# A pointwise convolution computed from seven quarter products, its weights loaded through a shared ring, and position terms of attention keys made once

## The chip, the core and the metric

The kernel runs on one core of a Trainium2 chip. The core has TensorE (PE: matrix products; its weight loads appear as PEld), VectorE (DVE), ScalarE (ACT), GpSimd (POOL) and SyncE (SP, which here issues nearly all DMAs). The time is that of one execution on the device in microseconds; the median of some runs is compared. Everything is float32.

## The reference

Two layers work on x, an array of 8 images with 512 channels of 32 x 32 pixels. Layer 0 is a bottleneck block with attention, layer 1 a depthwise and a pointwise convolution. Each adds its result to its input, which is group-normalised (32 groups) on the way in. Cut to what matters:

```python
def layer0(x):                       # C = 256, 4 heads of 64, N = 2
    t = silu(bn(conv1x1(x, cv1_w)))  # 512 channels
    ys = [t[:, :C], t[:, C:]]
    for i in range(N):
        yi = ys[-1]
        z = silu(bn(conv3x3(yi, m_cv1_w[i])))
        q, k, v = conv1x1(z, m_qkv_w[i])
        r = m_rw[i] + m_rh[i]        # one term per column, one per row
        a = softmax(q @ (k + r) * HD ** -0.5)
        z = silu(bn(conv1x1(a @ v, m_cv2_w[i])))
        ys.append(yi + z)
    return silu(bn(conv1x1(concat(ys), cv2_w)))

def layer1(x):
    h = relu(bn(depthwise3x3(x) + dw_b))
    h = where(max(abs(h)) over the image < 4, 0, h)         # per channel
    h = relu(bn(conv1x1(h, pw_w) + pw_b))                   # 512 -> 512
    return where(max(abs(h)) over the image < 1e-3, 0, h)

x = x + layer0(group_norm(x));  x = x + layer1(group_norm(x))
```

## The kernel before

One image of 512 channels and 1024 pixels is held as four chunks of 128 partitions x 1024. All eight images run through one long instruction stream; the work of layer 1 for an image lies among that of layer 0 for the next image.

The order is written out by hand as strings. Each stage function puts its pieces into lists under short names (`add`, line 298), and `go` (301) takes pieces from the lists as the words of a plan say. `FIRST` (45) is image 0, `HEAD` (64) the first part of every later image (with layer 1 of the image before), `TAIL` (80) and `LAST` (87) the end of a middle image and of the last. `InOrder` (95) keeps every engine but POOL in exactly this order. So where a word stands decides what stands behind it on its engine's queue; because nearly all calls pass through the helper in line 105, the profile shows that line for most instructions and they are told apart by tiles.

Words that matter here:
- `c`, `y` with `ca`, `ya`: the first 1x1 convolution (`cv1`, 590) and its ends on ScalarE; `g gm gd gv gp gb ga` is the group norm ahead of it (429), with two tiny products on TensorE and a power on POOL.
- `d`, `P`, `Rc`, `R`, `B`, `E`, `Ez`: the 3x3 convolution in transformed form (`conv3`, 631). VectorE makes three components (`d`, twelve pieces, into `kr`, `vt` and `qy`), TensorE multiplies them with transformed weights (six `P`, one ring tile each), VectorE transforms back (`R`, `B`, `E`) and ScalarE ends it (`Ez`, into `z`). In image 0 the weights are transformed first (`ta`, `ti`, `to`, 313) and stored in DRAM.
- `k`, `ka`, `kp`, `v`, `va`, `q`, `qa`: keys, values and queries (787). A key chunk is ended in two steps, below.
- `s`, `e`, `p`, `w`: scores, exponentials, their sums over keys on VectorE, and products with values (857); `h`, `z`, `n`, `nr`, `ns`, `sc`, `nc`: joining halves, denominators, reciprocals, spreading them by DMA, scaling, and a range check on ScalarE.
- `m`, `ma`, `mr`: the 1x1 convolution after attention (963).
- `Q`, `K`, `r0` to `r3`, `u0`, `a0`, `x0` and so on: the last 1x1 convolution; in images 1 to 6 it is done with seven quarter products in place of eight (`quartered`, 1090), whose weight sums image 0 makes once (`cw`, `combine_weights`, 1059).
- `i`, `im`, `id`, `iv`, `ip`, `ib`, `b`, `bm`, `t`, `l`, `lr`, `lp`: layer 1 to the depthwise convolution and its pruning (486); its taps `t` are VectorE's.
- `o`, `oa`, `fr`, `f`: the pointwise convolution (531): products, ScalarE's normalisation, the largest value per channel, residual and store.

The pointwise convolution multiplies all four input chunks of `ht` by `wpw_sb`, a tile of 1 MB that stays in SBUF. Per image these are eight output banks (chunk m, half n) of four products each:

```python
nc.tensor.matmul(bank(m, n), wpw_sb[:, k, m * P : (m + 1) * P],
                 ht[k][:, n * 512 : (n + 1) * 512], start=(k == 0), stop=(k == KC - 1))
```

In the last image the pruning factor is multiplied into `wpw_sb` in place of `ht`, and the products are ordered by input chunk.

The keys get their position terms in two steps: VectorE adds the column term as it empties the bank (`columns`, 812), POOL then adds the row term in place (`lines`, 821).

Other weights pass through a ring of `NRING` = 4 tiles of 1 MB (`ring_sources`, 377, `ring_load`, 399): each product that empties a tile issues the next load on SP's queue. In image 0 the ring is held before the second layer's weights, which are not ready (`held`, word `rh`).

PSUM has two double banks (`ps_big`: scores, `P`, keys), three single banks (`ps_acc`: values, `m`, `o`, `y` and the quarter products) and one more (`ps_mm`). Work tiles of 128 x 1024 come from a pool of 11.

Of the kernel before, what the change touches and what calls it, by code (L numbers as in the profile page):

```python
# [10 lines left out]
F32 = mybir.dt.float32  # L11
# [18 lines left out]
NRING = 4  # L30
# [15 lines left out]
    g*4 gm g gd g gv g gp g gb ga gm gd gv ga c gp fo gb c ga ta0 ga ta0*2 ti0 fo ta2 ti0 ta2  # L46
    ti0 to0*2 c ca ta2 c rl ca ta1*3 ti1 to1*2 ti1*2 y ya y ti2 d*2 ya d ti2 to2 y ti2 to2 rl ya
    y d*3 ya P d Rc d R d*2 P Rc R d*2 P Rc R B*2 P Rc R P Rc R E P Ez B*2 Rc R E Ez X dw*2
    ta0*2 k*3 ka k kp ka ta0 v kp ti0 v va ti0 v ti0 v va ta1 q*2 qa ta1 q ta1 q qa s e s e p
    to0 s e p w to0 s e w*2 ti1*2 s e p ti1 p s e p w s*2 e p w to1 e w to1 p s e w ta2 s e w h  # L50
    z ta2 s e p*2 w ta2 s ti2 e p w s e w p ti2 s e w p ti2 to2 s e p w to2 s e p w s e w s e rh
    p w h z s e s w e p w s n e p w nr s e p w nr s nr e nc p s nr e ns w s e p w*2 nc s e p w h
    z s p e p s w s e s e w p sc e p*2 w sc s e p w*2 s e p w*3 h z n nr*4 ns Q nc*2 K sc dp sc
    m ma mr m ma mr m*2 ma mr ma mr Q d*3 K d*2 P d*4 P Rc R d Rc R d*2 P Rc R B*2 P Rc R B P B
    Rc R E Ez P Rc R E Ez k X dx k*3 ka*2 kp*2 v*2 q v*2 va*2 q qa q*2 qa s*2 e*2 p s e p w s
    cw*2 e w s p e s e w s e p cw*2 p w s e p*2 s e w s e w*2 p w h z s e w cw s e p cw s e w p
    w p g*2 s e p w s e w p s e g w s p g s w g*2 e*2 p w h z s e p s w e g p w s e p n w nr g
    nr s e s p w nr e s e p w nr s p e ns w nc w s e p w h s nc s e p w e p w s e p w z s e p w
    s sc e p w sc s e p w*3 h z n nr*2 Q nr*2 ns Q sc*2 nc m nc m ma mr ma mr m ma m ma mr gm mr
    gd Q gv u A Q x u i A x i gp i*2 Q gb ga*4 Q im id Q iv A Q x ip i*2 ib b bm t*3 Q A t*2 x  # L60
    i*2 t
# [3 lines left out]
    c*2 b im id bm c ca iv t ip t l t*2 lr ib b c bm ca b t y t*2 d y bm d ya d ya d*5 y P Rc ya  # L65
    R d*2 P Rc R d P d Rc R B P Rc R B P B Rc R E P Rc B Ez R E Ez y k*3 ya X k ka dp kp t lp ka
    t*2 kp t*2 v*2 va t l t v*2 va t*2 lr lp q*4 qa s qa s e*2 t p s t e w t p s e w p l s*2 w
    e*2 p w p s t e s w s e*2 w t s p e p w*2 h lr z s e p t w s e w s p s p e w*2 p s e*2 p w s
    t e s p*2 w s e w e t p w h z lp t s*2 e p e w s*2 n e w s p w nr s p e w p w nr e p nr e
    s*2 nr t p ns w*2 e*2 nc l lr p lp w nc h sc s*2 e z w*2 s e*2 p*2 s e p w*2 s e w s e p*2  # L70
    w*3 p h n o nr sc z nr*3 ns o oa o oa sc m sc oa m nc ma nc ma m ma mr m mr ma mr*2 d o d*3
    o d oa d o P d*2 Rc d*3 oa R P Rc d R oa fr P Rc P R B Rc B R f P Rc P B*2 Rc R*2 E o E Ez
    fr oa Ez o X f k oa fr f fr f dx k*2 ka k kp ka kp v*2 q va v*2 q*3 va qa*2 s e s*2 w e p e
    w p s e p w s*2 e*2 p*2 w s*2 e*2 w s g p e w*2 s e w p s*2 h g e g p z w s p w e*2 s w e
    g*2 s*2 w e w p e g p g p*2 s w*2 e p s e w h s*2 e*2 p z p w*2 s e p*2 n s w nr*2 g w nr e
    s e p w p s w e p s nc e nr w s ns e nc w s h s p w z e p w e p s e w s e p sc s w p e p w s
    sc e p w*3 h n nr*4 ns z
# [3 lines left out]
    nc r2 Q*2 K r0 Q sc Q m r0 r2 r0 sc nc K m*2 ma mr ma m r0 ma mr r1 Q r1 Q*2 ma mr r2 mr  # L81
    r1*2 u0 r2 a0 u1 gm a1 x0 gd Q x1 u0*2 r3 gv r3 gp r3 Q gb u0 r3 u0 Q u0 a0 ga a0 ga Q i*2
    x0*2 ga Q i u0 a0 i im id Q iv ip u1 x0 Q u1*2 ib u1 b a1 x1 bm Q ga u1 a1 t i t Q x1 u1 i
    a1 i t i t x1 t*2
# [3 lines left out]
    Q sc*2 nc*2 m ma m*2 ma m rg ma mr*2 ma mr*2 Q*2 A rg x i*2 Q im id iv ip ib b bm Q t Q A x  # L88
    i*2 Q im id t*3 iv ip t ib Q t b Q bm t*4 l lr t A Q x i*2 Q im lp id t iv ip t A ib t b bm
    Q t*2 A x t l lr x i*2 o lp o*4 im id t*2 o*2 iv ip t ib b bm o*2 t o*4 t o*3 t*2 l t lr t*2  # L90
    lp t*2 o t*2 o*5 t l o*2 lr lp o*3 oa*2 fr o f oa*2 fr f o*2 oa*2 o*2 fr f oa*2 fr f
# [34 lines left out]
def fast_kernel(  # L126
# [42 lines left out]
    pt = [const_tile([P, HW], f"pt{c}") for c in range(KC)]  # L169
# [22 lines left out]
    wpw_sb = const_tile([P, KC, C], "wpw_sb")  # L192
# [26 lines left out]

    raw = [[t.rearrange("p a b -> p (a b)")[:, : 6 * C2] for t in (qy, kr, vt)]]  # L220
# [7 lines left out]
    for l in range(2):  # L228
        for dy in range(3):
            load_raw(l, dy)  # L230

# [144 lines left out]

    def ring_sources():
        for b in range(B):
            for l in range(2):
                for i in range(6):  # L380
                    yield u_dram[l][i].rearrange("p a b c d -> p (a b c d)"), 2048
                yield wqkv[:, l].rearrange("p k o -> p (k o)"), 1536
                if b == l == 0:
                    for m in range(2):
                        yield w2[:, :, m * P : (m + 1) * P], 1024
            if 0 < b < B - 1:
                for i in range(2):
                    for p in range(2):
                        yield s_dram[p][i].rearrange("p q k o -> p (q k o)"), 512 * (3 + i)
                continue  # L390
            for m in range(KC):
                yield w2[:, :, m * P : (m + 1) * P], 1024

    sources = list(ring_sources())
    ring = []

    held = [len(sources) - 9, 0]

    def ring_load(n=1):
        for _ in range(n):  # L400
            if len(sources) <= held[0]:
                held[1] += bool(held[0])
                continue
            src = sources.pop(0)
            t = ringp.tile([P, 2048], F32, tag="ring", name="wring")
            o = t[:, : src[1]]
            if src[1] == 1024:
                o = o.rearrange("p (k o) -> p k o", o=P)
            nc.sync.dma_start(o, src[0])
            ring.append(t)  # L410
# [74 lines left out]

    def layer1_front(groups, last=False):
# [28 lines left out]
        def prune(c):  # L515
            positive(keep[c])
            if last:

                w = wpw_sb[:, c, :]
                nc.vector.tensor_scalar(w, w, keep[c], None, ALU.mult)  # L520
            else:
                nc.gpsimd.tensor_scalar(ht[c], ht[c], keep[c], 1.0, ALU.mult, ALU.mult)
# [8 lines left out]
    def layer1_back(b):  # L531
# [4 lines left out]
        def bank(m, n):  # L536
            if (m, n) not in banks:
                if b < B - 1:
                    banks[m, n] = bank_tile("ps_pw")
                elif m in (0, 3):  # L540
                    t = big_tile("ps_pw")
                    banks[m, 0], banks[m, 1] = t[:, 0, :], t[:, 1, :]
                elif (m, n) == (2, 1):
                    banks[m, n] = ps_mm.tile([P, 512], F32, tag="mm", name="ps_pw")
                else:
                    banks[m, n] = bank_tile("ps_pw")
            return banks[m, n]

        def part(m, n, ks):
            for k in ks:  # L550
                nc.tensor.matmul(
                    bank(m, n),
                    wpw_sb[:, k, m * P : (m + 1) * P],
# [5 lines left out]
        def close(m, n):  # L559
            if n == 0:  # L560
                box[m] = work_tile("pw")
            act(box[m][:, n * 512 : (n + 1) * 512], bank(m, n), AF.Relu, BN5 + m)
# [15 lines left out]
        if b < B - 1:  # L578
            add("o", *[lambda m=m, n=n: part(m, n, range(KC)) for m, n in every])
# [6 lines left out]
        add("oa", *[lambda m=m, n=n: close(m, n) for m, n in every])  # L586
# [199 lines left out]

    def qkv(l, by_input):
# [22 lines left out]
        full = [P, 4, F, F // 4]  # L810

        def columns(m):
            col = rw[:, l, m, :].rearrange("p (t r) -> p r t", r=4)
            nc.vector.tensor_tensor(
                phases(kr[:, m, :]),
                phases(flat(tiles.pop(m + 2))),
                col.unsqueeze(2).to_broadcast(full),
                ALU.add,
            )

        def lines(m):
            row = rh[:, l, m, :].unsqueeze(1).unsqueeze(3)
            kk = phases(kr[:, m, :])
            nc.gpsimd.tensor_tensor(kk, kk, row.to_broadcast(full), ALU.add)  # L824
# [24 lines left out]
        add("ka", *[lambda m=m: columns(m) for m in range(2)])  # L849
        add("kp", *[lambda m=m: lines(m) for m in range(2)])  # L850
# [238 lines left out]

    def quartered():  # L1090
# [128 lines left out]
    for b in range(B):  # L1219
        first, last = b == 0, b == B - 1  # L1220
        if first:
# [8 lines left out]
            add("rl", *[lambda: ring_load(2)] * 2)  # L1230
            add("dw", lambda: nc.sync.dma_start(wm2_sb, wm2), lambda: nc.sync.dma_start(wpw_sb, wpw))

            def released():
                held[0] = 0
                ring_load(held[1])

            add("rh", released)
# [481 lines left out]
```

## Time and profile before

| | |
|---|---|
| median of 3 runs | 2625.31 us (2624.21 to 2625.61) |
| profiled execution, its time | 2622.91 us |
| profiled execution, its span | 2621.1 us |
| TensorE busy | 2578.2 us, 98% |
| VectorE busy | 2020.8 us, 77% |
| ScalarE busy | 1179.0 us, 45% |
| POOL busy | 169.9 us, 6% |
| mean DMA rate | 90 GB/s |
| granted TensorE clock | 0.998 |
| one middle image (910.89 to 1230.35) | 319.46 us, TensorE busy 319.17, VectorE 250.16 |

The page gives, for each engine, the busy time and the number of instructions; then groups of instructions by what they write and read, with busy time, mean length of one and the idle time ahead of them. A float32 product is two records, each with its weight load. Records of one engine can overlap a little, so the spacing of their starts is shorter than their length. The view by stage gives busy times in a stretch; the timeline lists merged instructions by their start; a wait is given with the instruction that ended it. The profiled execution ran 2.4 us below the median of the runs.

### The profile page before, as it was taken

What the parts mean: (1) busy time and instruction counts of PE and PEld (TensorE: products, weight loads), DVE (VectorE), ACT (ScalarE), POOL (GpSimd) and SP (SyncE); (2) the same over time, 40 slices, a digit from 0 to 9 for tenths busy, and PEclk for the clock granted to TensorE, in tenths of its full rate; (3) what the DMA queues carried; (4) which work ended last, traced back from release to release, by engine and by line L of the source; (5) the groups of instructions that cost most, each with busy time, mean ns of one, the idle gap of its engine ahead of it and who ended that gap; (6) DMA issues with size and microseconds to landing.
All of it is one profiled execution on the core that took longest, in us unless ns stands there. A gap on an engine that the chain in (4) does not pass through costs nothing.

```text
span 2621.1 us, 36162 instructions
## 1 busy us (share of the span) xinstructions
PE 2578.2 (98%) x14862; PEld 1328.7 (51%) x14862; DVE 2020.8 (77%) x2844; ACT 1179.0 (45%) x1509; POOL 169.9 (6%) x99
## 2 busy tenths in 40 slices
PE   8999999999999999999999999999999999999997
PEld 5454464634646346463464635645355544646443
DVE  8876588766887778778787778876788767887557
ACT  3634446253453544525445354444445444363534
POOL 1000011000100001000010000100001000010000
PEclk9999999999999999999999999999999999999999
DMA  9443130402304113040130402304122131302200
GB/s 340 157 154 124 65 141 25 151 31 73 138 20 149 31 67 141 17 165 17 64 141 17 165 17 80 125 27 155 33 95 95 61 121 33 132 27 85 73 17 34
DMA packets 74238, 236.00 MB, mean 90 GB/s; under 512 B 6096, under 2 KB 34000, under 8 KB 59984
## 3 DMA queue, kind: packets, MB, share of 16 engines
q1 hardware_dynamic: 70512, 230.19, 25.2%
q10 hardware_dynamic: 3552, 3.41, 0.4%
q8 instruction: 119, 1.95, 0.3%
q14 instruction: 55, 0.45, 0.1%
HBM read 183.77 MB, written 33.03 MB: 83 GB/s over the span
## 4 chain that ended last, share of the span: by engine, by line
PE 90%; DVE 4%; ACT 3%; issue 1%; DMA 0%; POOL 0%; SPq 0%; POOLq 0%; DVEq 0%; ACTq 0%
PE ps_av L105 16%; PE ps_s L105 15%; PE ps_c L105 12%; PE ps_cv L105 10%; PE ps_qk L105 8%; PE ps_cv2q L105 8%; PE ps_pw L105 8%; PE ps_v L105 4%; PE ps_m L105 4%; PE ps_y L105 4%; PE ps_dn L105 1%; DVE ht L105 1%; ACT qy L105 1%; ACT e L105 0%; ACT over L105 0%
## 5 line engine op out<-in xcount | busy, mean ns | idle before, releaser
L105 ACT ACTIVATE e<-ps_s 128x1024 f32<-128x1024 f32 x512 | 510.6, 1023 | 272.7 <-PE ps_s L105 262.2
L105 PE MATMUL ps_s<-qy,kr 64*64 64x512 f32 x4096 | 537.9, 592 | 4.4 <-ACT e L105 3.1
L105 PE MATMUL ps_av<-e,vt 64*64 64x512 f32 x4096 | 536.3, 590 | 1.4 <-ACT part L105 0.7
L105 DVE TENSOR_TENSOR sum<-sum,e 128x1024 f32<-128x1024 f32 x384 | 472.8, 1231 | 61.4 <-ACT e L105 42.0
L105 DVE SCALAR_TENSOR_TENSOR ht<-xn,v_sb,ht 128x961 f32<-128x961 f32 (+1 forms) x256 | 326.7, 1283 | 8.5 <-ACT ht L105 5.0
L105 PEld LDWEIGHTS ps_av<-e,vt 64*64 64x64 f32 x4096 | 183.9, 133 | 271.2 <-issue 237.5
L105 PEld LDWEIGHTS ps_s<-qy,kr 64*64 64x64 f32 x4096 | 173.6, 132 | 281.5 <-issue 169.8
L105 PE MATMUL ps_pw<-ht,wpw_sb 128*128 128x512 f32 x512 | 226.7, 598 | 5.4 <-DVE wpw_sb L105 5.4
L105 PE MATMUL ps_qk<-z,wring 128*128 128x512 f32 x512 | 227.2, 593 | 2.7 <-ACT z L105 1.9
L105 DVE TENSOR_TENSOR sum<-e 128x1024 f32<-128x1024 f32 x64 | 78.2, 1223 | 162.7 <-ACT e L105 162.7
L105 PEld LDWEIGHTS ps_pw<-ht,wpw_sb 128*128 128x128 f32 x512 | 96.5, 191 | 127.8 <-issue 126.0
L105 ACT COPY c<-ps_c 128x256 f32<-128x256 f32 x96 | 35.7, 372 | 272.6 <-PE ps_c L105 239.2
L105 PEld LDWEIGHTS ps_qk<-z,wring 128*128 128x128 f32 x512 | 96.8, 190 | 115.3 <-issue 106.6
L824 POOL TENSOR_TENSOR kr<-kr,v_sb 128x1024 f32<-128x1024 f32 x32 | 75.8, 2370 | 993.6 <-DVE kr L105 993.6
L105 DVE RECIPROCAL r<-ps_dn 128x128 f32<-128x128 f32 x128 | 113.4, 924 | 18.3 <-PE ps_dn L105 18.1
L105 PEld LDWEIGHTS ps_c<-kr,wring 128*128 128x128 f32 x1024 | 116.8, 192 | 8.3 <-issue 7.4
L105 PE MATMUL ps_c<-vt,wring 128*128 128x128 f32 x1024 | 117.2, 275 | 3.5 <-issue 1.9
L105 PEld LDWEIGHTS ps_c<-vt,wring 128*128 128x128 f32 x1024 | 115.6, 192 | 3.8 <-issue 3.8
L105 PE MATMUL ps_c<-kr,wring 128*128 128x128 f32 x1024 | 117.3, 275 | 0.2 <-ACT kr L105 0.2
L105 PE MATMUL ps_c<-qy,wring 128*128 128x128 f32 x1024 | 117.0, 275 | 0.0
L105 PE MATMUL ps_cv<-pt,w_sb 128*128 128x512 f32 x256 | 116.2, 605 | 0.0
L105 PE MATMUL ps_v<-wring,z 128*128 128x256 f32 x512 | 114.6, 380 | 1.1 <-DVE kr L105 1.1
(165 smaller groups left out, 3176.5 us busy)
## 6 DMA issues: line engine op xcount, KB each, us to landing
wring<-u SPq DMA_DIRECT2D x96, 1024.0 KB, 4.8
pt<-in_x SPq DMA_DIRECT2D x32, 512.0 KB, 6.1
rw<-r SPq DMA_DIRECT2D x64, 256.0 KB, 3.4
xt<-in_x SPq DMA_DIRECT2D x32, 512.0 KB, 6.2
out<-xt SPq DMA_DIRECT2D x32, 512.0 KB, 2.9
wring<-in_wqkv SPq DMA_DIRECT2D x16, 768.0 KB, 4.2
wring<-s SPq DMA_DIRECT2D x12, 1024.0 KB, 4.8
wring<-s SPq DMA_DIRECT2D x12, 768.0 KB, 4.7
```

Of the source, the lines that this page charges most:

```text
L105: made = method(*args, **kwargs)
L824: nc.gpsimd.tensor_tensor(kk, kk, row.to_broadcast(full), ALU.add)
```

## The change

The pointwise convolution of images 0 to 6 takes the form of `quartered`: the 512 x 512 weight matrix and the 512 x 1024 input are cut into quarters, and seven products of quarters take the place of eight. VectorE forms four differences of the input's quarters (`ot`, into the tiles `pt`, which hold the normalised input of the next image until then). The products run for both halves of the rows of each output quarter (`o` and `O`); ScalarE copies the first (`ok`, `Ok`), VectorE adds the others up (`ou`, `Ou`), in part back into the bank, and ScalarE closes each quarter as before (`oa`, `Oa`). The sums of weight quarters are made in image 0 (`combine_more`, three more words `cw`), stored in DRAM and loaded through the ring, 896 KB for each half. The last image keeps the plain product; its weights are also loaded through the ring. The 1 MB tile `wpw_sb` goes, and the ring has five tiles.

The position terms of the keys (`r`) are added up once per layer and chunk in image 0 on POOL (`rk`) and stored in DRAM. In each layer, SP loads them into `kr` (`kd`) when the convolution's products have freed it, and VectorE adds them to the bank in one plain addition. POOL's step `kp` goes.

The load of the next image into `pt` (`dp`) moves behind the pointwise products. The four plans are written anew; only a part of `HEAD` is shown.

```diff
-NRING = 4
+NRING = 5
 FIRST (part)
-    g*4 gm g gd g gv g gp g gb ga gm gd gv ga c gp fo gb c ga ta0 ga ta0*2 ti0 fo ta2 ti0 ta2
-    ti0 to0*2 c ca ta2 c rl ca ta1*3 ti1 to1*2 ti1*2 y ya y ti2 d*2 ya d ti2 to2 y ti2 to2 rl ya
-    y d*3 ya P d Rc d R d*2 P Rc R d*2 P Rc R B*2 P Rc R P Rc R E P Ez B*2 Rc R E Ez X dw*2
+    g*5 gm gd g*2 gv g gp gm gd gb ga gv ga c gp fo gb ga ta0 ga ta0*2 ti0 ta2 fo ta2 c to0 ti0
+    to0 c ti0 ta2 c rk*2 rl ca rk ta1*3 rk y ya ti1 ca ti2 to2 ti1*2 y to1 ya ti2 to1 d y*2 ti2
+    d*2 ya d to2 rl P Rc d*2 R d*2 P d Rc d kd R d P Rc R ya B d P B P Rc R Rc R P E B Ez B Rc R
 HEAD (part)
-    w*3 p h n o nr sc z nr*3 ns o oa o oa sc m sc oa m nc ma nc ma m ma mr m mr ma mr*2 d o d*3
-    o d oa d o P d*2 Rc d*3 oa R P Rc d R oa fr P Rc P R B Rc B R f P Rc P B*2 Rc R*2 E o E Ez
-    fr oa Ez o X f k oa fr f fr f dx k*2 ka k kp ka kp v*2 q va v*2 q*3 va qa*2 s e s*2 w e p e
+    s nr t p ns l w e p*2 w lr lp w ot h s e s w p ot s w ot s e*2 p*2 e w p s w e w s e p*2 z
+    sc w nc w*2 h n nc o O nr ok Ok sc z nr*3 ns o ou oa O*2 Ou sc m Oa m sc nc m ma m ma mr ma
+    ot mr ma mr o nc mr d ou Ou o O d ou Ou o d O ou*2 oa Ou*2 d Oa o O P d*2 Rc d*3 R P kd d*2
+    Rc d R P Rc P R B Rc P B Rc P R B*2 Rc R ou E oa Ou R Oa o O dp E Ez*2 X k v*2 k ou oa Ou
+    fr*2 Oa ka fr f*2 fr f*2 dx va k v*2 va k q*2 ka q qa q qa s e s*2 e p e w p s e p w s*2 e*2
...
 def ring_sources():
     for b in range(B):
         for l in range(2):
+            if b and l:
+                for p in range(2):
+                    yield q_dram[1][p].rearrange("p q k o -> p (q k o)"), 1792
...
+    yield wpw.rearrange("p k o -> p (k o)"), 2048
...
+def by_quarters(rights, names, pairs):
+    src, sums = rights
+    b11, b12, b21, b22 = (
+        (lambda i=i, n=n: src[:, 2 * i : 2 * i + 2, n * 512 : (n + 1) * 512])
+        for i in range(2)
+        for n in range(2)
+    )
+    t1, t2, t3, t4 = ((lambda t=t: t.rearrange("p (k n) -> p k n", k=2)) for t in sums)
...
+    add(
+        names[0],
+        lambda: less(t1, b12, b11),
+        lambda: less(t2, b22, t1),
+        lambda: less(t3, b22, b12),
+        lambda: less(t4, b21, t2),
+    )
+    right = dict(a11=b11, a12=b21, s2=t2, s1=t1, s3=t3, a22=t4, s4=b22)
+    for kinds, finish in zip(names[1:], pairs):
+        one_pair(right, kinds.split(), finish)
+
+def one_pair(right, kinds, finish):
+    banks, kept, w = {}, [], []
+    def product(name):
+        if not w:
+            w.append(ring.pop(0)[:, :1792].rearrange("p (q k o) -> p q k o", k=2, o=P))
+        banks[name] = bank_tile("ps_q")
+        for k in range(2):
+            nc.tensor.matmul(
+                banks[name],
+                w[0][:, PRODUCTS.index(name), k, :],
+                right[name]()[:, k, :],
+                start=(k == 0),
+                stop=(k == 1),
+            )
+        if name == PRODUCTS[-1]:
+            ring_load()
+    def keep():
+        t = work_tile("kept")
+        kept.extend((t[:, :512], t[:, 512:]))
+        nc.scalar.copy(kept[0], banks["a11"])
+    def plus(o, x, name):
+        nc.vector.tensor_tensor(banks[name] if o is None else kept[o], kept[x], banks[name], ALU.add)
+    add(kinds[0], *[lambda name=name: product(name) for name in PRODUCTS])
+    add(kinds[1], keep)
+    add(
+        kinds[2],
+        lambda: plus(None, 0, "a12"),
+        lambda: plus(0, 0, "s2"),
+        lambda: plus(1, 0, "s1"),
+        lambda: plus(0, 0, "s3"),
+        lambda: plus(None, 1, "s3"),
+        lambda: plus(None, 0, "a22"),
+        lambda: plus(None, 1, "s4"),
+    )
+    ends = (("a12", 0, 0), ("s3", 1, 1), ("a22", 1, 0), ("s4", 0, 1))
+    add(kinds[3], *[lambda e=e: finish(banks[e[0]], *e[1:]) for e in ends])
...
         if b < B - 1:
-            add("o", *[lambda m=m, n=n: part(m, n, range(KC)) for m, n in every])
+            pairs = [lambda ps, low, n, p=p: close(2 * p + low, n, ps) for p in range(2)]
+            by_quarters((h_all, pt), ("ot", "o ok ou oa", "O Ok Ou Oa"), pairs)
...
+def positions(l, m):
+    t = work_tile("pos")
+    full = [P, 4, F, F // 4]
+    col = rw[:, l, m, :].rearrange("p (t r) -> p r t", r=4).unsqueeze(2)
+    row = rh[:, l, m, :].unsqueeze(1).unsqueeze(3)
+    nc.gpsimd.tensor_tensor(phases(t), col.to_broadcast(full), row.to_broadcast(full), ALU.add)
+    nc.sync.dma_start(r_dram[l][:, m], t)
...
-    def columns(m):
-        col = rw[:, l, m, :].rearrange("p (t r) -> p r t", r=4)
-        nc.vector.tensor_tensor(
-            phases(kr[:, m, :]),
-            phases(flat(tiles.pop(m + 2))),
-            col.unsqueeze(2).to_broadcast(full),
-            ALU.add,
-        )
-    def lines(m):
-        row = rh[:, l, m, :].unsqueeze(1).unsqueeze(3)
-        kk = phases(kr[:, m, :])
-        nc.gpsimd.tensor_tensor(kk, kk, row.to_broadcast(full), ALU.add)
+    def load_positions():
+        nc.sync.dma_start(kr, r_dram[l])
+    def add_positions(m):
+        nc.vector.tensor_tensor(kr[:, m, :], flat(tiles.pop(m + 2)), kr[:, m, :], ALU.add)
...
+def combine_more(i, src):
...
+    def load():
+        nc.sync.dma_start(w, src)
+        for name in ("a11", "a12", "a22"):
+            store(name)
...
+    add(
+        "cw",
+        load,
+        lambda: sums(("s1", "s2"), (("a21", "a22", ALU.add), ("s1", "a11", ALU.subtract))),
+        lambda: sums(("s3", "s4"), (("a11", "a21", ALU.subtract), ("a12", "s2", ALU.subtract))),
+    )
```

## The prediction

> **What bounds the kernel now.** I read the page's busy times first, then the busy times by stage, then TensorE's timeline in one image's stage of the pointwise convolution, then who TensorE waited for.
>
> ```profile
> span 2621.1 us, 36162 instructions
> ...
> PE 2578.2 (98%) x14862; PEld 1328.7 (51%) x14862; DVE 2020.8 (77%) x2844; ACT 1179.0 (45%) x1509; POOL 169.9 (6%) x99
> ...
> L105 PE MATMUL ps_pw<-ht,wpw_sb 128*128 128x512 f32 x512 | 226.7, 598 | 5.4 <-DVE wpw_sb L105 5.4
> ```
>
> TensorE is busy 2578.2 of 2621.1 us, so time falls only as its work falls, unless it begins to wait. The 256 pointwise products (two records each) take 226.7 us. By stage (columns: stretch, length, PE, PEld, DVE, ACT, POOL busy, clock, DMA share, GB/s):
>
> ```profile
> 776.51:832.48 55.97, 55.97 (x274) 36.84 (x274) 44.27 (x82) 17.33 (x32) 0.00 (x0) 1.00 0.35 120
> 14.00:57.00 43.00, 41.26 (x172) 24.64 (x171) 41.02 (x68) 20.21 (x31) 4.64 (x2) 1.00 0.97 364
> ```
>
> The first line is image 2's pointwise stage inside image 3's layers: TensorE never idles, VectorE is at 79%. The second is the start of image 0: VectorE at 95%, DMA at 97% with 364 GB/s, and TensorE already idles 1.7 us. TensorE's order in the first stretch:
>
> ```profile
> 776.44 10.57 PE L105 MATMUL ps_pw<-ht,wpw_sb 128*128 128x512 f32 x24
> 786.85 7.03 PE L105 MATMUL ps_m<-z,wm_sb 128*128 128x512 f32 x16
> 793.71 10.46 PE L105 MATMUL ps_pw<-ht,wpw_sb 128*128 128x512 f32 x24
> ```
>
> Starts give the price: 786.85 - 776.44 = 10.41 us for 12 products, 0.43 us a record, 0.86 us a product. The waits of the whole run:
>
> ```profile
> PE ps_pw L105 <- DVE wpw_sb L105: 5.4, 2, 4.7
> ...
> PE ps_s L105 <- ACT e L105: 3.1, 1, 3.1
> ```
>
> The first lies in the last image; the 3.1 us is one wait at 264.4, in image 0, where ScalarE stood in a range check (`nc`) that waited for VectorE's reciprocals. An image in the middle takes 319.47 us with 0.3 us of idle TensorE.
>
> **The change, part by part.** Prices from the groups kept apart by shape:
>
> ```profile
> L105 DVE TENSOR_TENSOR part<-part,ps_cv2q 128x512 f32<-128x512 f32 x36 | 24.5, 681 | 9.7 <-PE ps_cv2q L105 9.5
> L105 DVE TENSOR_TENSOR ucomp<-uplane 128x1024 f32<-128x1024 f32 x6 | 7.3, 1222 | 0.1
> L105 DVE TENSOR_TENSOR ht<-ps_cv,ht 128x1024 f32<-128x1024 f32 x2 | 2.4, 1222 | 1.5 <-PE ps_cv L105 1.5
> L105 DVE TENSOR_TENSOR kr<-ps_qk,v_sb 128x1024 f32<-128x1024 f32 x32 | 63.6, 1992 | 41.1 <-PE ps_qk L105 41.1
> ```
>
> *Products.* Images 0 to 6 have 28 products instead of 32: 4 x 0.858 = 3.43 us, all on TensorE's path; 7 x 3.43 = **-24.0 us**. Image 7 keeps the plain product.
>
> *VectorE, per image.* Added: four differences of 128x1024 (1.22 us, the second row) = 4.9, fourteen additions of 128x512 (0.68) = 9.5. Removed: four key ends at 1.99 become plain additions of a bank and a tile at 1.22, 3.1 less. Together +11.3 on 250.2 us of 319.5, some 83% of the shorter image: no bound as a mean. ScalarE gets two copies of 0.58 us against 55% idle: nothing.
>
> *The local price.* Nearly all new additions stand between the attention of layer 0 and the scores of layer 1, beside the second 3x3 convolution, which is full of VectorE work. I walk the new order there with measured spacings: records that follow each other on VectorE start closer than they last (a `d` step 1.25, an `R` 1.33, a `B` 1.28, an `E` 0.6, an addition 0.62 us). As a check, in the profile from the fourth `mr` (794.73) to the last `E` (828.68) are 33.95 us; the spacings give 32.6 and the waits before it 1.1. In the new order that stretch loses one `fr` and one `f` (2.6) and gains ten additions (6.2): 36.2 us of VectorE. TensorE has, from the end of the four `m`, seven products (12.0), six `P` (21.4), two products (3.4): 36.9 us until `k` needs `z`, and after the last `E` ScalarE still needs 1.2 us for `Ez`. Two waits come of it. (1) Only three accumulator banks serve the products and `m`; one is held by a product (`s2`) whose addition is due after `mr`, so the third `m` waits for the first `ma`, and before that stands a table load of 1.28 us: 0.55, and 0.1 more at `s1`. (2) `Ez` stands on ScalarE behind the two closings `oa`, `Oa`, which wait for additions, so `k` starts some 0.45 late; queued behind `k` are `v`, `q` and the scores. Sum 1.1, of which 0.2 was there before: 0.9 an image, 7 x 0.9 = **+6.3 us**. Ends: 0 (the records overlap better than I walk) and 2.0 (every addition at its full 0.68 and one more late bank).
>
> VectorE writing a sum back into PSUM, as eight additions an image do, has no row. Below: 0.68, as for PSUM read. Above: twice that, one more pass. I take the nearest row, 0.68. [...] the rows say 681 ns with a bank and 689 without, so nothing is added. [...]
>
> *Weights through the ring.* Two loads of 896 KB an image and one MB for positions per layer: 19 + 16 MB on 236 MB, where DMA is a quarter busy. `kd` stands on SP's queue behind the ring load for the second `P` and waits for what that product frees, so it holds only the next ring loads; these are four products (14 us) ahead, with a fifth buffer, and a 1 MB ring load lands in 4.8 us. `dp`, moved behind the pointwise products because the differences live in `pt`, is needed by the statistics some 30 us later and lands in 6.1. Nothing; if a ring load were late, its 4.8 us.
>
> *Keys.* The POOL additions `kp` go: scores wait for queries made later, so no gain on the path; VectorE's taps beside them get shorter. How much is seen here, taps on VectorE:
>
> ```profile
> 382.38 1.21 DVE L105 SCALAR_TENSOR_TENSOR ht<-xn,v_sb,ht 128x961 f32<-128x961 f32 x1
> ...
> 385.87 5.66 DVE L105 SCALAR_TENSOR_TENSOR ht<-xn,v_sb,ht 128x992 f32<-128x992 f32 x3
> ```
>
> and the additions on POOL:
>
> ```profile
> 382.61 2.82 POOL L824 TENSOR_TENSOR kr<-kr,v_sb 128x1024 f32<-128x1024 f32 x1 [42.41 <-DVE kr L105]
> ...
> 386.50 2.89 POOL L824 TENSOR_TENSOR kr<-kr,v_sb 128x1024 f32<-128x1024 f32 x1
> ```
>
> Three taps took 5.66 where three take 3.6: two POOL additions cost VectorE 2 us, 1 us each.
>
> *Image 0.* Four such additions (`rk`) now run on POOL right after the `pow` that ends at 18.6, while VectorE makes the transformed weights that the third `P` waits for (1.58 us idle at 52.0). By the row 4 x 1 = 4 us of VectorE. [...] I take the row, 4.0, less one `d` step (1.25) that the new order moves behind this `P`: 2.7. The 2 MB of position stores meet full DMA queues: at 390 GB/s 5.4 us, of which 2.6 fit into the slack between 20 and 32 us; the 2.8 left delay the same `P`, so they lie beside the 2.7. The start: eight statistics now precede the first `gp`, which puts `nb` behind the second means, and the first product 0.9 later. Against it, `nc` moves far behind the scores, and the 3.1 us wait goes. Image 0: 0.9 + 2.7 - 3.1 = **+0.5 us** (-3 to +8). The seventeen further stores and eight small additions for quarter weights lie under attention, where `cw` already did.
>
> **Sum.** -24.0 + 6.3 + 0.5 = -17.2 us on a span of 2621.1: 2603.9. The profiled execution took 2622.9, 1.8 around its span; the median of the runs is 2.4 more, 2625.3. So **2608 us**.
>
> **Rivals.** (A) The order hides everything: no new wait in the stages, image 0 gains 1: 2625.3 - 25 = 2600. For it: the old order, as dense, idles 0.3 us an image. Against it: VectorE's stretch is then as long as TensorE's. (B) [...] with late ring tiles for 3 more: +7.5 and 6.3 on -24: 2615. For it: VectorE 95% and DMA 97% busy there. Against: the row of 1 us. (C) Slower: additions that write PSUM. Four of them (`s3`, `a22` of each pair) stand in the full stretch; if one costs more than 0.68 + (3.43 - 0.9)/4 = 1.3 us, the stage is worth nothing. At 2.0 us an image loses 0.9 + 5.3 - 3.43 = 2.8: 7 x 2.8 + 0.5 = +20, 2645. Against: bank reads show no such price. (D) The saving fails to appear because the quarter products are dearer: their weights change every product as before, one load per 128x512, and 191 ns of load lie under 429: no reason.
>
> **How the numbers follow.** Forecast 0.52 (2604 to 2613), A 0.26, B 0.14, C 0.04, D or the unforeseen 0.04, half of it no change. A measurement tells 0.2%, 5.3 us. Leaving out C, D and the tails of A and B: 2599 to 2617. Faster 0.92 (forecast, A, B), same 0.04, slower 0.04.
>
> **What would show it.** Right: 28 products, 56 records fewer, so 14806 TensorE records; 319.5 us an image becomes about 317; VectorE near 260 an image; TensorE waits for ScalarE's `m` and `z` at `m` and `k`. If no wait shows there, A. If the third `P` of image 0 starts after 58 us, B. If additions with a bank as output are over 1 us, C. I am wrong altogether if attention, where the differences are put, makes the denominators late.

## The result and the profile after

The changed kernel takes **2612.27 us** (2611.65 to 2612.56), the kernel before, run beside it, 2624.76 (2624.14 to 2625.61): a ratio of 0.9952, interval 0.9935 to 0.9969. The forecast was 2608, with a range of 2599 to 2617. The number lies inside, but not because the working held: one step was 11 us too low, 4 us came back at two other places (waits forecast too dear, and a shorter wait at the end that was not forecast), and 2.6 us more of the agreement is chance. The profiled execution of before ran 2.4 us below its median, that of after 0.3 above; between the two spans, which is what the sum forecast, the difference is 10.3 us and not 17.2.

The page, after:

```profile
span 2610.8 us, 36350 instructions
...
PE 2561.2 (98%) x14806; PEld 1292.4 (50%) x14806; DVE 2081.7 (80%) x2978; ACT 1185.3 (45%) x1523; POOL 101.7 (4%) x71
```

TensorE's records are 56 fewer, as forecast; its busy time fell by 17.0 us, the span by less. Groups kept apart by shape (count, busy us, mean ns, idle time before):

```profile
L104 PE MATMUL ps_q<-pt,wring 128*128 128x512 f32 x224 | 100.3, 595 | 0.6
L104 DVE TENSOR_TENSOR kr<-ps_qk,kr 128x1024 f32<-128x1024 f32 x32 | 39.1, 1223 | 47.0 <-PE ps_qk L104 47.0
L104 DVE TENSOR_TENSOR ps_q<-kept,ps_q 128x512 f32<-128x512 f32 x56 | 38.3, 693 | 13.6 <-PE ps_q L104 7.8 <-issue 5.7
L104 DVE TENSOR_TENSOR kept<-kept,ps_q 128x512 f32<-128x512 f32 x42 | 27.5, 684 | 0.7
L104 DVE TENSOR_TENSOR pt<-ht,pt 128x1024 f32<-128x1024 f32 x14 | 17.0, 1216 | 0.0
L886 POOL TENSOR_TENSOR pos<-v_sb 128x1024 f32<-128x1024 f32 x4 | 12.1, 3030 | 9.0 <-DMA r<-pos 8.4 <-DVE uplane L104 0.6
```

A quarter product costs what a plain one did (595 against 598 ns a record). A sum written back into PSUM takes 693 ns, one written to SBUF 684: the unknown price of the forecast is settled at its lower end. POOL's four position sums took 3.03 us each, where the 32 additions of row terms before took 1.96 to 2.90, 2.37 as a mean.

Busy time by stage (stretch, length, PE, PEld, DVE, ACT, POOL, clock, DMA share, GB/s): image 2's pointwise stage up to the keys, the start of image 0, two stretches inside image 0, and a middle image:

```profile
784.21:837.75 53.54, 52.94 (x266) 35.29 (x265) 47.06 (x89) 15.64 (x31) 0.00 (x0) 1.00 0.37 130
14.00:57.00 43.00, 33.52 (x84) 17.00 (x85) 39.40 (x47) 19.16 (x24) 16.83 (x6) 0.90 0.85 313
48.24:58.48 10.24, 5.75 (x27) 5.75 (x28) 7.50 (x12) 3.68 (x6) 0.00 (x0) 0.50 1.10 381
249.62:256.45 6.83, 4.94 (x24) 1.54 (x28) 6.69 (x9) 2.96 (x3) 0.00 (x0) 0.50 0.66 208
1076.75:1393.20 316.45, 316.20 (x1847) 159.88 (x1844) 257.73 (x370) 145.38 (x189) 10.69 (x7) 1.00 0.27 96
```

The pointwise stage went as hoped: TensorE stays busy but for 0.6 us, VectorE at 88%, and an image takes 316.45 us. The start did not: where TensorE was busy 41.26 of 43 us, it now is 33.52, and twice in image 0 the granted clock is 0.5, for 10.24 and 6.83 us. TensorE's timeline after, in image 0 and in image 2's stage:

```profile
52.73 10.14 PE L104 MATMUL ps_c<-kr,wring 128*128 128x128 f32 x64 [9.06 <-DVE kr L104]
...
784.21 7.13 PE L104 MATMUL ps_q<-ht,wring 128*128 128x512 f32 x16
791.18 1.88 PE L104 MATMUL ps_q<-pt,wring 128*128 128x512 f32 x4
792.90 7.03 PE L104 MATMUL ps_m<-z,wm_sb 128*128 128x512 f32 x16
799.77 12.53 PE L104 MATMUL ps_q<-pt,wring 128*128 128x512 f32 x28
812.14 7.31 PE L104 MATMUL ps_c<-kr,wring 128*128 128x128 f32 x64
```

The first `P` of image 0 waited 9.06 us for VectorE, and the 64 records that take 7.31 us later took 10.14. Who TensorE waited for in the run:

```profile
PE ps_c L104 <- DVE kr L104: 9.1, 1, 9.1
...
PE ps_s L104 <- ACT e L104: 4.4, 1, 4.4
```

The old 3.1 us wait at 264.4 is gone, as forecast; a new one of 4.45 us stands at 251.5. Set side by side by the start of the same product (the first that sums denominators), the two traces say where the 10.3 us come from:

| place | before | after | after less before |
|---|---|---|---|
| first product of all | 13.39 | 14.42 | +1.0 |
| first `P` of image 0 | 42.71 | 52.73 | +10.0 |
| last denominators of image 0 | 275.74 | 287.09 | +11.4 |
| first of image 1 | 431.88 | 443.33 | +11.5 |
| last of image 7 | 2507.21 | 2498.03 | -9.2 |
| end | 2621.12 | 2610.79 | -10.3 |

Image 0 loses 11.5 us, the seven stages with quarter products gain 20.6, and the tail 1.2 (the wait in the last image is 3.5 us instead of 4.7).

### The profile page after: what moved, and what is told of

Its sections match the earlier page's. It is cut to its first block, busy times and chain, and to the rows that moved or that the text cites. A ratio compares the mean times of both kernels' runs of the same rounds, so it can differ in the third digit from the quotient of the medians.

```text
span 2610.8 us, 36350 instructions
## 1 busy us (share of the span) xinstructions
PE 2561.2 (98%) x14806; PEld 1292.4 (50%) x14806; DVE 2081.7 (80%) x2978; ACT 1185.3 (45%) x1523; POOL 101.7 (4%) x71
## 3 DMA queue, kind: packets, MB, share of 16 engines
q10 hardware_dynamic: 3552, 3.41, 0.4%
## 4 chain that ended last, share of the span: by engine, by line
PE 91%; DVE 6%; ACT 1%; DMA 1%; issue 0%; SPq 0%; POOL 0%; ACTq 0%; DVEq 0%
PE ps_av L104 17%; PE ps_s L104 16%; PE ps_c L104 12%; PE ps_cv L104 10%; PE ps_qk L104 8%; PE ps_cv2q L104 8%; PE ps_q L104 6%; PE ps_v L104 4%; PE ps_m L104 4%; PE ps_y L104 4%; PE ps_dn L104 1%; DVE ht L104 1%; ACT qy L104 1%; DVE vtmp L104 1%; DVE mid L104 1%; DVE uplane L104 0%
## 5 line engine op out<-in xcount | busy, mean ns | idle before, releaser
L104 ACT ACTIVATE e<-ps_s 128x1024 f32<-128x1024 f32 x512 | 509.5, 1023 | 291.5 <-PE ps_s L104 264.4
L104 PE MATMUL ps_s<-qy,kr 64*64 64x512 f32 x4096 | 514.9, 593 | 5.8 <-ACT e L104 4.4
L104 PE MATMUL ps_av<-e,vt 64*64 64x512 f32 x4096 | 507.2, 591 | 0.0
L104 DVE SCALAR_TENSOR_TENSOR ht<-xn,v_sb,ht 128x961 f32<-128x961 f32 (+1 forms) x256 | 312.5, 1228 | 8.4 <-ACT ht L104 5.0
L104 PEld LDWEIGHTS ps_s<-qy,kr 64*64 64x64 f32 x4096 | 160.4, 133 | 295.0 <-issue 185.5
L104 PEld LDWEIGHTS ps_av<-e,vt 64*64 64x64 f32 x4096 | 164.8, 133 | 279.1 <-issue 270.5
L104 PEld LDWEIGHTS ps_c<-qy,wring 128*128 128x128 f32 x1024 | 115.8, 192 | 1.6 <-issue 0.9
L104 PE MATMUL ps_m<-z,wm_sb 128*128 128x512 f32 x256 | 112.5, 592 | 0.0
L104 PE MATMUL ps_y<-pt,w_sb 128*128 128x512 f32 x256 | 112.3, 592 | 0.0
```

The source lines that it names most:

```text
L104: made = method(*args, **kwargs)
```

## Experiments

Four explanations for the 11.5 us of image 0 were on the table: POOL's position sums hold VectorE up (4 us of VectorE in the forecast); their stores fill the DMA queues; the making of the quarter weights disturbs attention; or the new order itself is at fault. From the fifth run on, "theory 1" is that each loss comes from where the work of the first three stands. "After" below is 2612.27 us.

**1. The old position terms in the new order.**

```diff
-        add("kd", load_positions)
-        add("ka", *[lambda m=m: add_positions(m) for m in range(2)])
+        add("ka", *[lambda m=m: columns(m) for m in range(2)])   # as before
+        add("kp", *[lambda m=m: lines(m) for m in range(2)])     # as before
-            add("rk", *[lambda l=l, m=m: positions(l, m) for l in range(2) for m in range(2)])
```

> The changed kernel with the key positions done as before: the column term on VectorE, the row term on POOL, no position sums in image 0, no stores of them and no loads. If the positions cost image 0 its 9 us ahead of the first product of the 3x3 convolution (additions on POOL holding VectorE, or their stores), that product starts near 43.5 us in place of 52.7, TensorE's clock stays full there, and the time is 2612.3 - 9.2 - 2.9 = about 2600 us. If the new order of image 0 is to blame, the product starts near 52 us and the time stays at 2612 us.

Measured: 2632.44 us (2631.11 to 2634.28), 1.0028 of before (1.0019 to 1.0037). The first `P` starts at 44.50, there is no half clock there, and by the end of image 0 only 3 us are lost: the order alone does not make the 10 us at the first `P`. But the expected time was missed widely, since every later image takes about 320.5 us instead of 316.5. The waits of this run:

```profile
PE ps_qk L104 <- ACT vt L104: 12.9, 7, 1.9
...
PE ps_qk L104 <- DVE kr L104: 7.7, 7, 1.1
PE ps_v L104 <- DVE kr L104: 4.8, 10, 1.7
```

Three waits at the keys come back in each of seven images, 25.4 us in all. VectorE's column step takes 1.98 us where the plain addition takes 1.22, and in layer 0 POOL's step stands beside the taps. So in this dense order the position part is worth 4 us an image; the forecast's "no gain on the path" was true only of the old order.

**2. POOL fills the position tiles without reading.** Loads and stores stay.

```diff
-        nc.gpsimd.tensor_tensor(phases(t), col.to_broadcast(full), row.to_broadcast(full), ALU.add)
+        nc.gpsimd.memset(t, 0.25)
```

> The four position sums of image 0 become writes of a constant on POOL; stores, loads and the plain addition stay, so the position terms are left out. If it is POOL's reading of SBUF that holds VectorE (two inputs each), VectorE's 8.7 us of lengthened instructions disappear, the first product of the 3x3 convolution starts near 44 us and the time is about 2601 us. If the 2 MB of stores in full DMA queues are to blame, it starts near 52 us still and the time stays near 2611 us.

Measured: 2604.15 us (2603.49 to 2606.45), 0.9921 (0.9905 to 0.9938): 8.1 us below after, but some 3 above the 2601 expected. VectorE is where it shows. First after, VectorE and POOL in image 0:

```profile
19.36 5.64 DVE L104 TENSOR_TENSOR uplane<-wtmp,vt 128x512 f32<-128x512 f32 x2
...
26.18 2.41 DVE L104 TENSOR_TENSOR sc<-sc,v_sb 128x24 f32<-128x24 f32 x1
...
37.62 3.40 DVE L104 SCALAR_TENSOR_TENSOR uplane<-vt,wtmp 128x512 f32<-128x512 f32 x2
...
18.74 5.71 POOL L886 TENSOR_TENSOR pos<-v_sb 128x1024 f32<-128x1024 f32 x2
25.08 3.47 POOL L886 TENSOR_TENSOR pos<-v_sb 128x1024 f32<-128x1024 f32 x1 [0.63 <-DVE uplane L104]
36.96 2.91 POOL L886 TENSOR_TENSOR pos<-v_sb 128x1024 f32<-128x1024 f32 x1 [8.41 <-DMA r<-pos]
```

and with the memset, the first of these steps and one ahead of the first `P`:

```profile
19.49 1.29 DVE L104 TENSOR_TENSOR uplane<-wtmp,vt 128x512 f32<-128x512 f32 x2
...
42.22 1.29 DVE L104 SCALAR_TENSOR_TENSOR vtmp<-yp 128x512 f32<-128x512 f32 x2 [2.81 <-DMA r<-pos]
```

In the kernel before, the three VectorE rows took 1.29, 0.18 and 1.29 us. The additions of 24 numbers took 2.41 us because they could not end before POOL's third sum did. The excess is 4.35 + 2.23 + 2.11 = **8.7 us** for four sums: VectorE instructions with two SBUF inputs stood still while POOL's sums read SBUF. A POOL instruction that only writes (the memsets, 0.95 us each, lie beside the first step too) did not hold them: that step took its 1.29 us. The last line is the rest of the miss: the stores are still there, VectorE waits 2.81 us for one of them, and the first `P` starts at 47.53, not near 44.

**3. The sums made, but not stored.** The loads read another tensor, so keys get other positions.

```diff
-        nc.sync.dma_start(r_dram[l][:, m], t)
-            nc.sync.dma_start(kr, r_dram[l])
+            nc.sync.dma_start(kr, wpw.rearrange(...))
```

> POOL makes the four position sums as in the changed kernel, but they are not stored, and the key tile is loaded from other data of the same size, so the position terms are left out. If POOL's additions hold VectorE, the lengthened instructions stay and the first product starts at 50 to 52 us; the time is 2609 to 2612 us. If the stores are to blame it starts near 44 us and the time is near 2601 us.

Measured: 2610.99 us (2609.8 to 2611.06), 0.9945 (0.9928 to 0.9961). The first `P` starts at 50.98, 1.75 us sooner than after; VectorE's long steps are as long as after (5.66 and 2.42 us), and the half clock stays for 6.83 us. The stores are worth 1 to 3 us (1.3 of the time here, the wait of 2.81 in run 2), the sums the rest.

**4. No quarter weights are made.** The ring loads slices of the plain weights instead, so the pointwise results are others; all else stays.

```diff
-                        yield q_dram[1][p].rearrange("p q k o -> p (q k o)"), 1792
+                        yield wpw.rearrange("p k o -> p (k o)")[:, 256 * p : 256 * p + 1792], 1792
-            combine_more(1, wpw)
+            add("cw", *[lambda: None] * 3)
```

> The quarter weights of the pointwise convolution are not made in image 0: no load, eight additions and fourteen stores there, and the ring loads other data of the same size, so the pointwise weights are left out. If their stores delay the next weights' load, the 4.45 us wait of the scores at 251.5 and the half clock after it (about 2.5 us) go: 2612.3 - 6.9 = about 2605 us. If the wait has to do with the range check as in the kernel before, it stays and the time is 2611 to 2612 us.

Measured: 2604.41 us (2604.0 to 2605.22), 0.992 (0.9904 to 0.9937): 7.9 us below after, as expected, and the wait at 251 us with its half clock is gone. What stood there, after (SyncE's issues, then VectorE and ScalarE):

```profile
230.42 3.33 SPq L104 DMA_DIRECT2D q<-ht  x6
233.86 3.94 SPq L104 DMA_DIRECT2D q<-scomb  x8
237.85 0.55 SPq L104 DMA_DIRECT2D ht<-in_w  x1
...
243.82 0.69 DVE L104 TENSOR_TENSOR scomb<-ht 128x512 f32<-128x512 f32 x1 [5.49 <-DMA ht<-in_w]
...
250.43 1.94 ACT L104 ACTIVATE e<-ps_s 128x1024 f32<-128x1024 f32 x2 [5.67 <-DMA s<-scomb]
```

Fourteen stores of quarter weights take 7.4 us of SyncE's queue. The load of the last layer's weights stands behind them, VectorE's sum of those weights waits 5.49 us for it, and behind that sum in VectorE's fixed order stand the sums of exponentials. ScalarE then waits 5.67 us for the store that ends the chain, and the scores wait for ScalarE. The queue is not all of the delay: the load fills the tile from which the first six stores read, so it could not be issued before the last of these had landed, at 235.23; the eight stores behind them held it 2.6 us more. And run 4 takes load, additions and stores away together, so it does not tell them apart.

**5. Position sums in other places.** Layer 0's go to the very start, layer 1's behind the last denominators of layer 0.

```diff
 FIRST
-    g*5 gm gd ... c rk*2 rl ca rk ta1*3 rk y ya
+    rk*2 g*5 gm gd ... c rl ca ta1*3 y ya
-    ... n z nr*4 ns Q nc*2 K
+    ... n z nr*4 ns Q rk*2 nc*2 K
```

> The POOL position sums of layer 0 are moved to the very start, where VectorE only gathers statistics, and those of layer 1 behind the first attention's output scaling; nothing is left out. If the sums lengthen VectorE only by being beside its two-input steps (theory 1), the third-component steps return to about 1.3 us, the first P starts near 48 and the time falls by 6 to 9 us from 2612.3, to 2603 to 2606. If the stores on full DMA queues are what delays P (rival), the stores still fall into the load of the input, P stays at 51 to 53 and the time stays at 2610 to 2612; moved ahead of the statistics, they may even delay the first product by 1 to 3 us.

Measured: 2609.98 us (2608.46 to 2610.58), 0.9947 (0.9932 to 0.9962). The first `P` starts at 46.65 instead of 52.73, sooner than expected, but the time was missed by some 5 us. The losses moved along with the sums:

```profile
9.07 2.31 DVE L104 TENSOR_TENSOR d<-d 128x2 f32<-128x2 f32 x1
...
144.30 2.94 DVE L104 TENSOR_TENSOR z<-z,rw 128x512 f32<-128x512 f32 x1
147.17 3.47 DVE L104 TENSOR_TENSOR sum<-sum,e 128x1024 f32<-128x1024 f32 x1
```

At the start the second sum (9.0 to 11.4) holds a squaring of 128 x 2 numbers, 0.16 us of work, for 2.31; the first product comes 2.2 us later. In attention the layer 1 sums hold a 0.69 and a 1.22 us step for 2.3 us each, and TensorE waits 3.44 us for the denominators. The statistics of the group norm beside the first sum, which have one input, kept their 0.68 to 0.69 us. So the mechanism was shown again and the choice of place was bad: POOL started as soon as a tile was free, not where the word stands.

**6. Weight sums of the last 1x1 convolution spread further back.**

```diff
-    ... s p w s p e*2 w cw*2 w*2 p s w h e w z s p s e*2 p w s p g cw e s e w s w s p e g
+    ... s p w s p e*2 w*3 p s w h e w z s p s cw e*2 p w s cw p g e s e w s w s p cw e g
```

> In image 0 the six weight sums of the second set are spread further back in the attention of layer 1, so that their stores do not stand in front of the weight load for the next sums; nothing is left out. If the queue of stores ahead of that load is the cause of the 4.45 us wait at 251 us and of the half clock behind it (theory 1), both go: 4.45 + 2.5, about -6 us, so 2606. If the sums cost by their VectorE work, or by the space that they take (rival), the wait only moves and the time stays within 2 us of 2612.3.

Measured: 2606.28 us (2604.82 to 2606.95), 0.9935 (0.992 to 0.995): 6.0 below after, no wait and full clock at 251 us, the time as expected. (The second set is here that of the last convolution; in run 10 it is the pointwise one.) The reason was another than the one expected, for the move leaves the fourteen stores ahead of the load, and the load as late as it was:

```profile
229.44 3.38 SPq L104 DMA_DIRECT2D q<-ht  x6
232.91 3.94 SPq L104 DMA_DIRECT2D q<-scomb  x8
236.90 0.55 SPq L104 DMA_DIRECT2D ht<-in_w  x1
...
242.80 0.69 DVE L104 TENSOR_TENSOR scomb<-ht 128x512 f32<-128x512 f32 x1 [1.42 <-DMA ht<-in_w]
```

The load lands 5.9 us after its issue, as in after. What moved is VectorE's sum that needs it: sums of exponentials now stand ahead of this sum, which waits 1.42 us in place of 5.49, and nothing that TensorE needs is late behind it. So the 4.45 us wait came of the place of that sum in VectorE's order, given a late load; the store queue alone does not make it. Whether the same work still costs something there is open: the time is 1.9 above run 4, and the two intervals overlap.

**7. Additions ahead of a `d`.**

```diff
-    ot mr ma mr o nc mr d ou Ou o O d
+    ot mr ma mr o nc mr ou Ou d o O d
```

> In every later image one VectorE step d of the convolution moves behind the first two additions ou, Ou of the pointwise products; nothing is left out. If the stretched pair of records at product s1 of the second half waits for the bank that these additions free (theory 1), its spacing of 678 + 534 ns returns to 429 + 429, at 0.35 us an image: -2.5 us in all, 2609.8. If the spacing is a slower fetch of something (rival), it stays and the time stays at 2612.3; if d then comes late for the first P behind it, a new wait of up to 0.6 us an image shows there and the time rises to 2614 to 2616.

Measured: 2611.87 us (2610.34 to 2613.14), 0.9954 (0.9939 to 0.997): no difference that can be told. The stretched pair of records is gone (the spacing of 678 + 534 ns is 429 + 429), so it was a wait for an accumulator bank that these additions free. But the 0.35 us come back: 0.06 at a later product, and 0.4 in two steps at the second component's `P`, whose banks VectorE's back-transformation empties 0.14 us later than after (the last such step ends at 1136.04 and 1139.90, `P` goes on at 1136.14 and 1140.00). An image takes 316.53 us, against 316.45 to 316.97 after. In this stretch VectorE's time is short, not a bank.

**8. The three moves together**, with the statistics at the start in the order of the kernel before.

> The three moves together (position sums early, weight sums later, additions ahead of d), with the statistics of the start in the order of the kernel before. Theory 1 (each loss is a matter of place): 2612.3 - 8 - 6 - 2.5 - 1 = 2595, between 2592 and 2599. If only the additions' move works: 2610; if only the image 0 moves work: 2597 to 2600. If image 0 loses the gain again further on (rival: the losses hide each other), 2603 or above.

Measured: 2605.21 us (2600.99 to 2608.53), 0.9929 (0.9916 to 0.9943), ten above the 2595 of theory 1 and in the range named for the rival that the losses hide each other. That they hide each other does not follow: alone the moves gave 2.3, 6.0 and 0.4, together 8.7, and here, in runs of a wide spread, 7.1. What was wrong are the 8 and the 2.5 put in for the moves of runs 5 and 7; the 3.2 us wait for the denominators at 153.6 was still there.

**9. Layer 1's position sums written into the key tile.** The rest as in run 8, without the move of run 7.

```diff
-        t = work_tile("pos")
+        t = kr[:, m, :] if l else work_tile("pos")
```

> As the run with all three moves, but without the additions' move, and the position sums of layer 1 are written into the key tile itself once the scores of layer 0 have read it, so that POOL cannot start them while VectorE sums exponentials; nothing is left out. Theory 1 (the sums cost what they overlap of VectorE's two-input steps): the 3.2 us wait of the denominators at 153 us goes, the sums fall where VectorE waits for TensorE, and the time is 2602 (2600 to 2604). Rival (the stores and loads of positions are what costs): the wait only moves towards the first P of layer 1, and the time stays at 2605 or above.

Measured: **2601.36 us** (2600.35 to 2602.9), 0.9913 of before (0.99 to 0.9927), 10.9 below after and as expected: the lowest median of the kernels that leave nothing out, though its interval overlaps that of run 8. Its POOL sums and its wait for denominators:

```profile
117.81 3.51 POOL L886 TENSOR_TENSOR kr<-v_sb 128x1024 f32<-128x1024 f32 x1 [96.37 <-PE ps_s L104]
148.73 3.07 POOL L886 TENSOR_TENSOR kr<-v_sb 128x1024 f32<-128x1024 f32 x1 [27.41 <-issue]
```

```profile
PE ps_dn L104 <- DVE sum L104: 1.0, 2, 0.8
```

The first sum was released by scores that read the tile; for the second, 31 us later, the profile names no releaser. They do not fall where VectorE waits, as was expected: each meets one VectorE step (3.47 and 3.19 us instead of 1.22, the second a sum of exponentials). But they no longer come one behind the other, and of the 3.2 us wait 0.8 is left.

**10. Neither positions nor quarter weights made.**

> Neither the position sums and their stores nor the second set of weight sums are made in image 0; all loads stay, from other places of DRAM, so positions and pointwise results are not the reference's. What is left is the gain of the products, less the waits of the later stages. If the two costs of image 0 add up (theory 1): 2612.3 - 8.2 - 7.9 less up to 3 for the stores: 2593 to 2596. If they hide each other: 2600 or above. From the steps of the forecast the same kernel would be 2625.3 - 24.0 + 6.3 + 0.9 - 3.1 = 2605; with the 2.9 that the trace shows for the later stages 2602 less the tail's 1.2.

Measured: 2595.15 us (2594.12 to 2596.17), 0.9887 (0.9872 to 0.9902): 17.1 below after. The parts measured alone, 8.1 for reading sums and 7.9 for quarter weights, make 16.0; the stores are the likely rest. The two costs of image 0 add up, and with them gone the change would have been worth 29 us. Run 9 leaves about 6 of the 17. The time also lies 6 to 10 us below the 2601 to 2605 that the forecast's own steps give. Part of this is in image 0: its last denominators start at 270.29, 5.45 us ahead of before, where the forecast's other terms (first product 0.9 late, a `d` step of 1.25 moved, the 3.1 us wait gone) make 3.45.

## Why the prediction was right or wrong

**Products, -24.0: right.** 56 records fewer, and a spacing of 429 ns between undisturbed ones: 0.858 us a product, 3.43 an image.

**Unknown price of a sum into PSUM: right**, 693 ns; the case in which these additions make the kernel slower has no ground.

**VectorE per image: right**, 257.7 us in an image where about 261 were forecast.

**Waits of the stages, +6.3: the mechanism was half right, the size wrong.** Measured is 24.0 - 20.6 = 3.4. The forecast's largest term, 0.55 at the third `m` behind a table load, did not come: in the trace the load (793.56) ran before ScalarE had any `m` to end. At `s1`, where 0.1 was forecast, are 0.35 in each image; at `k`, where 0.45 was, about 0.1; and in two images a wait of 0.5 and 0.34 us stands at a sixth `P`, which the walk did not name. The walk found the stretch where VectorE is short, and run 7 confirms that, but not the places.

**Image 0, +0.5: wrong by 11, in three steps.**

*"By the row 4 x 1 = 4 us of VectorE."* It was 8.7. The row had been misread. Two POOL additions lay in its stretch, and the 2 us were shared between both. But beside the first, VectorE worked mostly on a bank, and one of the three taps met a POOL step that is no addition, before:

```profile
383.94 2.04 DVE L105 TENSOR_TENSOR kr<-ps_qk,v_sb 128x1024 f32<-128x1024 f32 x1 [0.28 <-PE ps_qk L105]
385.41 1.12 POOL L522 TENSOR_SCALAR ht<-ht,keep 128x1024 f32<-128x1024 f32 x1
387.60 2.81 DVE L105 SCALAR_TENSOR_TENSOR ht<-xn,v_sb,ht 128x961 f32<-128x961 f32 x1
```

The first step has one SBUF input and took no longer than usual (mean 1.99). The tap behind it, beside `ht<-ht,keep`, took 1.69 us instead of 1.21; the next, beside the second addition, 2.81. So the one addition that held a tap cost 1.6 us, not 1: read pair by pair, the row gives 6.4 us for four, an estimate, and not 4. A position sum reads other data, took 2.40 to 2.44 us where it came first (runs 3 and 5), and held VectorE for 2.1 to 2.2: four of them are the 8.7. The forecast also laid the stores beside the sums, at no price of their own (its 390 GB/s is the rate of before from 32 to 38 us, 391); in run 3 they are 1.75 us on top at the first `P`.

Rival B, which put 7.5 us on image 0 by the author's estimate, described this part, and its mark, a third `P` after 58 us, holds (62.7); its 7.5 still fell short of 11.5. By that mark it was the better account, and its 2615 lies nearer to 2612.3 than the forecast's 2608.

*"The seventeen further stores and eight small additions for quarter weights lie under attention."* The bytes do, but the step named only the bytes. It left out what hangs on them: a weight load behind the stores, a VectorE sum that needs it, and behind that sum VectorE's sums of exponentials. The 4.45 us wait goes when the weights are not made (run 4), and also when, with the same stores and the same load, only the sum is placed later (run 6).

*A wait was priced at its length.* Both waits brought half clock with them, which began inside the wait and went on behind it: 2.8 us more for the first 64 records of `P`, and about half of TensorE's 4.94 us at 250, some 2.5. No step had this.

The two right ones of this part: the start was 1.0 late where 0.9 was forecast, and the 3.1 us wait went. First `P` 10.0, slow clock 2.8 and 2.5, wait 4.45, less 3.1, make 16.6; image 0 ended 11.5 late. Some 3.6 of the difference are shorter waits at other `P`, keys and values (7.4 us before, 3.8 after); about 1.5 I did not place.

**Sum.** 11.0 (image 0) less 2.9 (stage waits) less 1.2 (tail, not forecast) is the 6.9 us by which the span was missed.

## What to carry to other kernels

One-off work in the first image is not free because it is small: price it by what it holds up, on an engine and on a queue, not by its own microseconds. When a row is to give the price of a collision, look at which of its instructions can collide at all, here by how many inputs from SBUF they have (two: a pair of steps took 5.64 us beside POOL's sums and 1.29 without; one: a step took 0.68 to 0.69 either way), before dividing by their number. A move that shares an engine's time differently only moves a wait, while a move to where the work behind has slack (run 6, in part run 9) takes it away.

## What the runs showed of the hardware

The half clock does not follow from the length of a wait. In each of the twelve traces the changes of the granted clock, as far as TensorE still works, lie whole multiples of 3.413 us apart (after: half at 48.24 and 249.62, 59 such steps apart, full again three steps, 10.24 us, and two steps, 6.83 us, later). What the next step brings goes with how long TensorE idles within the present one. Before and after, by such steps (columns as above; the length less the first busy time, PE's, is the idle time):

```profile
259.32:262.74 3.42, 2.00 (x20) 0.46 (x12) 3.42 (x5) 0.00 (x0) 0.00 (x0) 1.00 0.00 0
262.74:266.15 3.41, 1.73 (x16) 0.67 (x20) 2.29 (x2) 3.38 (x7) 0.00 (x0) 1.00 0.59 150
...
246.21:249.62 3.41, 0.85 (x8) 0.00 (x0) 3.31 (x5) 0.00 (x0) 0.00 (x0) 1.00 0.89 305
249.62:253.04 3.42, 1.53 (x8) 0.55 (x12) 3.32 (x4) 1.94 (x2) 0.00 (x0) 0.50 0.90 267
253.04:256.45 3.41, 3.41 (x20) 0.99 (x16) 3.38 (x6) 1.02 (x1) 0.00 (x0) 0.50 0.42 148
```

All steps of the twelve traces, from the first record of the clock (17 to 22 us after the start) to the last product:

| clock in the step | TensorE idle in it, us | clock in the next step |
|---|---|---|
| full | up to 1.92 | full |
| full | 2.04 to 3.41 (24 cases) | half |
| half | up to 0.29 (24 cases) | full |
| half | 0.65 to 3.41 (12 cases) | half |

So a wait counts by how the steps cut it. The 3.10 us of before at 264 (1.42 and 1.68), the 3.08 of run 2 at 47 (1.80 and 1.28) and a wait of 3.48 in the last image of run 10 (1.92 and 1.56) brought no half clock; the 3.23 us of run 8 at 154, with 2.97 in one step, did. The 4.48 us of run 2 at 244 brought one step and the 4.45 of after at 251 two; but a part of these two lay in the wait itself, so in TensorE's work at half clock they differ by 3.41 against 4.94 us, which is 0.8 us of time. A small move ahead of such a wait can seem to gain or lose more than it does.
